# Two outlook-attention layers: channels dealt out as 3p+i over the partitions, and layer 1's results turned by VectorE in 32 by 32 pieces

## The chip, the cores and the metric

The kernel runs on one core of one Trainium2 chip, in float32 throughout. The metric is the device time of one execution in microseconds (us). The kernel is a single launch; weights are only reordered on the host.

## The reference

The input x is 8 images of 56 x 56 positions with 384 channels. Two layers follow each other, each with a residual.

```python
def _gn(v, G=32, eps=1e-5):                       # 32 groups of 12 channels
    g = v.reshape(B_, H_, W_, G, C_ // G)
    m = jnp.mean(g, axis=(1, 2, 4), keepdims=True)
    s = jnp.var(g, axis=(1, 2, 4), keepdims=True)
    return ((g - m) / jnp.sqrt(s + eps)).reshape(v.shape)

# layer 0, on x = _gn(x): 12 heads of 32 channels, 3 x 3 patches
v = einsum('bhwc,oc->bhwo', x, Wv)
attn = softmax(einsum('bhwc,oc->bhwo', x, Wa).reshape(b, n, 12, 9, 9) * 32 ** -0.5, axis=-1)
out = einsum('bnhpq,bnqhd->bnphd', attn, patches(v))   # 9 outputs per position ...
y = fold(out)                                          # ... added up where they overlap
x = x + einsum('bhwc,oc->bhwo', y, Wo)

# layer 1, on _gn(x): 6 heads of 64 channels, one output per position
a = softmax((x @ W_attn + b_attn).reshape(B, H * W, 6, 9), axis=-1)
y = einsum('bpKhd,bphK->bphd', patches(x @ W_v + b_v), a)
x = x + y @ W_proj + b_proj
```

## The kernel before

**Layout.** Images go in pairs: a column of a pair is 2 x 56 = 112 rows. Between the layers and for every projection, activations lie with channels on the partitions, 128 to each of three chunks (`NCH` = 3): channel 128i + p is on partition p of chunk i. The input and the output have channels innermost in DRAM, so a column is turned on the way in and on the way out.

**Layer 0** takes one column of one pair per step, 224 steps. In `stats_chunk` TensorE transposes the raw x of the next pair, four columns and one chunk at a time (`pt`, from `xr`), ScalarE copies the result to `xt`, VectorE takes `bn_stats`, and `xt` is kept in DRAM. `norm_params` makes scale and bias of a pair: `bn_aggr` over each chunk and image, then `over_groups` twice (the mean, then the variance), each a matrix product with `gmat`. A group of 12 channels straddles chunks, so `gmat` has a block for each neighbouring pair of chunks and each product is seven float32 matmuls, which the trace shows as 14 instructions. `normed` applies scale and bias with one instruction per chunk and image. `attend` projects to logits (three banks of 288 columns) and to values, `fold` and the DRAM tables `ztab` and `vtab` bring softmax weights and values into patch form, and `plan` queues for each patch column of 7 the contractions (`pc`), their copies to `yT` by ScalarE, and six `project_out` (two halves of columns by three chunks), whose results go to DRAM as layer 1's input together with their statistics.

**Layer 1** works on 32 groups of 7 columns (4 pairs of 8), one column per step. A step runs one job of a queue, then `attend` for its column (a matmul of 438 columns for logits and values, of which every eighth column has none, since 8 columns of 112 rows fill 7 tiles of 128), then one more job, then stores logits and values by DMAs from POOL. The order of the jobs is the order of the work on TensorE: every matmul is kept in program order, and in layer 1 VectorE's, ScalarE's and SP's instructions too. `weigh`, `share` and `move` make the softmax of a group and its patch form at steps 3, 4 and 5 of the next group. `fetch` (at step 0) reads the `z` and `vp` patches of the group before by DMAs from SP, and queues 14 jobs, due from step 3: for each of two images two pairs of contractions (`pc`, two tiles of PSUM, `NC` = 2), each followed by a job that turns one column back, then six `project_out`, the last three with a turn attached. `project_out` multiplies `yT` by the output weights into `po`, and VectorE adds bias and residual in place in `x1t`. `turn(m)` transposes the three chunks of one column of `x1t` with TensorE into PSUM, ScalarE copies the turned column to `ot`, and after columns 3 and 6 POOL issues the DMA to the output. Turns of columns 3 to 6 wait in the list `turning` until the next group's contractions.

**PSUM** [...] three `banks` in rotation, the tags `t`, `f` and `o`, and two for `c`. In layer 1 `attend` rotates over two of the `banks`, the third serves every second turn; `project_out` alternates between `o` and `f`, and `move` uses `f`.

**Helpers.** Line 118 is every matmul, line 121 every transpose, and line 133 every instruction recorded through `InOrder`, so in the profile they are told apart by their tiles.

Of the kernel before, what the change touches and what calls it, by code (L numbers as in the profile page):

```python
# [15 lines left out]
def two_outlook_layers(  # L16
# [81 lines left out]

    xf = x.rearrange("b y x c -> (b y) x c")
# [52 lines left out]
    near = [range(max(0, i - 1), min(NCH, i + 2)) for i in range(NCH)]  # L152
    gmat = [const.tile([P, len(near[i]), P], F32, name=f"gmat_{i}") for i in range(NCH)]
    with tc.tile_pool(name="ps_setup", bufs=2, space=PS) as ps_setup:
        gsel = yT_flat[:G, :C]
        gpsimd.memset(gsel, 1.0)
        gpsimd.affine_select(
            out=gsel, in_=gsel, compare_op=ALU.is_ge, fill=0.0,
            base=0, pattern=[[1, C]], channel_multiplier=-GC,
        )  # L160
        gpsimd.affine_select(
            out=gsel, in_=gsel, compare_op=ALU.is_ge, fill=0.0,
            base=GC - 1, pattern=[[-1, C]], channel_multiplier=GC,
        )
        for i in range(NCH):
            pg = ps_setup.tile([P, C], F32, tag="pg", name=f"pg_{i}")
            matmul(pg, gsel[:, i * P : (i + 1) * P], gsel, start=True, stop=True)
            lo, hi = near[i][0] * P, (near[i][-1] + 1) * P
            nc.vector.tensor_scalar_mul(gmat[i].rearrange("p j c -> p (j c)"), pg[:, lo:hi], 1.0 / GC)
# [93 lines left out]
    def weight(pool, src, n, name, queue=nc.sync):  # L263
        t = pool.tile([P, NCH, n], F32, name=name)
        queue.dma_start(t, src.rearrange("(i p) n -> p i n", p=P))
        return t

    def norm_params(st, name, params, key):

        mv = stat.tile([P, NCH, IMG, 2], F32, tag="mv", name=f"mv_{name}")  # L270

        def over_groups(src, what):
            pg = ps.tile([P, NCH, IMG], F32, tag="t", name=f"p{what}_{name}")
            for j in range(NCH):
                for i in near[j]:
                    matmul(
                        pg[:, j, :], gmat[i][:, j - near[i][0], :], src[:, i, :],
                        start=(i == near[j][0]), stop=(i == near[j][-1]),
                    )
            g = stat.tile([P, NCH, IMG], F32, tag=what, name=f"{what}_{name}")  # L280
            vector.tensor_copy(g, pg)
            return g

        for i in range(NCH):
            for b in range(IMG):
                vector.bn_aggr(mv[:, i, b, :], st[:, i, b, :, :])
        yield
        mean = over_groups(mv[:, :, :, 0], "gmean")

        part = stat.tile([P, NCH, IMG], F32, tag="part", name=f"part_{name}")  # L290
        vector.tensor_sub(part, mv[:, :, :, 0], mean)
        vector.tensor_mul(part, part, part)
        vector.tensor_add(part, part, mv[:, :, :, 1])
        yield
        var = over_groups(part, "gvar")
        std = stat.tile([P, NCH, IMG], F32, tag="std", name=f"std_{name}")
        scalar.activation(std, var, AF.Sqrt, bias=eps_t)
        scale = const.tile([P, NCH, IMG], F32, name=f"scale_{name}")
        vector.reciprocal(scale, std)
        bias = const.tile([P, NCH, IMG], F32, name=f"bias_{name}")  # L300
        vector.scalar_tensor_tensor(bias, mean, -1.0, scale, ALU.mult, ALU.mult)
        params[key] = scale, bias
        yield
# [90 lines left out]
    scalar.dma_start(bo_t, bo1.rearrange("(i p) -> p i", p=P))  # L394
# [25 lines left out]
    def layer0(late, pools):  # L420
# [22 lines left out]
        def stats_chunk(pair, blk, i):  # L443

            if blk == 0 and i == 0:
                stats[pair] = stat.tile([P, NCH, IMG, NBLK, 6], F32, tag="st0", name=f"st0_{pair}")
# [7 lines left out]
            for j in range(XB):  # L454
                transpose(pt[:, j, :], xr[:, j, i * P : (i + 1) * P], ident[:R, :R])
            scalar.copy(xt[:, i], pt)
            yield
            for b in range(IMG):
                vector.bn_stats(stats[pair][:, i, b, blk, :], xt[:, i, :, b * H : (b + 1) * H])
# [54 lines left out]
        for blk in range(NBLK):  # L514
# [5 lines left out]
            if blk == 1:  # L520
                wv_t = weight(fixed, wv0, C, "wv0_t", sync)
# [31 lines left out]
        scalar.dma_start(wn, wa0.rearrange("(i p) n -> p i n", p=P))  # L553
# [21 lines left out]
        def normed(g, chunks, whole=True, shared=True, both=False):  # L575

            scale, bias = params[g // NBLK]
            xin, to = xins[g], xns[g // 2 % 2]
            for i in chunks:
                for b in range(IMG):  # L580
                    rows = slice(b * H, (b + 1) * H)

                    def put(dst, src):
                        if both and b:
                            vector.tensor_scalar(
                                dst, src, scale[:, i, b : b + 1], bias[:, i, b : b + 1],
                                ALU.mult, ALU.add,
                            )
                            return
                        scalar.activation(  # L590
                            dst, src, AF.Identity,
                            bias=bias[:, i, b : b + 1], scale=scale[:, i, b : b + 1],
                        )

                    n = XB - g % 2
                    if whole:
                        put(to[:, i, g % 2 * XB : g % 2 * XB + n, rows], xin[:, i, :n, rows])
                    if shared and g % 2:
                        put(
                            to[:, i, :, R + b * PART : R + (b + 1) * PART],  # L600
                            xin[:, i, n, rows].rearrange("p (j y) -> p j y", j=NTILE),
                        )
# [188 lines left out]
        def plan(pair, px, first, second, last):  # L791
# [38 lines left out]
            if px == 0:  # L830
                st1s[pair] = stat.tile([P, NCH, IMG, 2 * NPX, 6], F32, tag="st1", name=f"st1_{pair}")

            def project_out(half, j):
# [11 lines left out]
                for b in range(IMG):  # L845
                    vector.bn_stats(
                        st1s[pair][:, j, b, 2 * px + half, :],
# [30 lines left out]
        def upkeep(step):  # L878

            pair, c = divmod(step, W)  # L880
            if pair == 0:
                if c == 1:
                    gpsimd.memset(wts, 0.0)
                if c == 3:
                    sync.dma_start(wo_t, wo0.rearrange("(i p) n -> p i n", p=P))
# [11 lines left out]
            if j < NCH and g < NPAIR * NBLK:  # L897
                normed(g, (j,))
            if step < NCH:
                normed(1, (step,), shared=False)  # L900
# [13 lines left out]
        for i in range(NCH):  # L914
            normed(0, (i,), both=True)
            normed(1, (i,), whole=False, both=True)
# [81 lines left out]
    def layer1(pools, base, last_of_layer0, late_w):  # L998
# [24 lines left out]
        def normed(g, m0, m1):  # L1023
# [4 lines left out]
            for lo, hi in ((first + m0, min(cut, first + m1)), (cut, first + m1)):  # L1028
# [3 lines left out]
                for i in range(NCH):  # L1032
                    for b in range(IMG):
                        rows = slice(b * H, (b + 1) * H)
                        scalar.activation(
                            to[:, i, :, rows], x1ts[g][:, i, lo - first : hi - first, rows],
                            AF.Identity,
                            bias=bias[:, i, b : b + 1], scale=scale[:, i, b : b + 1],
                        )
# [7 lines left out]
        nc.gpsimd.dma_start(wc_t[:, :, :NA1], wa1.rearrange("(i p) n -> p i n", p=P))  # L1047
        nc.gpsimd.dma_start(wc_t[:, :, NA1:], wv1.rearrange("(i p) n -> p i n", p=P))
# [4 lines left out]
        wo_t = weight(fixed, wo1, C, "wo1_t")  # L1053
# [3 lines left out]
        def attend(g, m):  # L1057
# [7 lines left out]
            pa = bank(P, 0, NC1, 2)  # L1065
# [77 lines left out]
        def fetch(g, due):  # L1143
# [10 lines left out]
            for b in range(IMG):  # L1154
# [20 lines left out]
                for t in range(0, (NPY1 + n_tile - 1) // n_tile, NC):  # L1175
                    jobs.add(due, lambda t=t, f=contract: [f(t + n) for n in range(NC)])

                    jobs.add(due, turning.pop(0) if turning else lambda: None)

            def project_out(half, j):  # L1180
                lo, hi = HALVES[half]
                n = (hi - lo) * R
                po = ps.tile([P, 4 * R], F32, tag="of"[(half * NCH + j) % 2], name=f"po1_{g}_{half}_{j}")
# [6 lines left out]
            def turn(m):  # L1190

                half = m // 4
                lo, hi = HALVES[half]
                if m == lo:
                    fetch.ot = io.tile([R, 4, C], F32, tag="ot", name=f"ot_{g}_{half}")
                pt = banks[-1][:R, :C] if m % 2 else ps.tile([R, C], F32, tag="t", name=f"pt1_{g}_{m}")
                for i in range(NCH):
                    transpose(pt[:, i * P : (i + 1) * P], x1t[:, i, m, :], ident)
                scalar.copy(fetch.ot[:, m - lo, :], pt)
                if m == hi - 1:  # L1200
                    nc.gpsimd.dma_start(  # L1201
                        of[pair * R : (pair + 1) * R, px * PX + lo : px * PX + hi, :],
                        fetch.ot[:, : hi - lo],
                    )

            out, back = project_out, turn
            for work_of in (
                (lambda: out(0, 0),), (lambda: out(0, 1),), (lambda: out(0, 2),),
# [96 lines left out]
```

## Time and profile before

| | us |
|---|---|
| runs (median of 3; lowest to highest) | 3314.91; 3310.96 to 3317.94 |
| the profiled execution's own time | 3315.84 |
| its span, first to last instruction | 3314.0 |
| TensorE busy with matmuls | 3183.7 |
| VectorE, ScalarE, POOL busy | 1870.4, 1366.3, 1565.1 |
| layer 1's transposes of results (312 + 234 + 72 + 54 instructions) | 51.5 + 38.6 + 12.0 + 8.9 |
| ScalarE's copies to `ot` (128 + 96) | 61.2 + 46.1 |
| matmuls `pgmean` and `pgvar` (112 + 112) | 17.7 + 20.3 |
| mean granted TensorE clock | 0.978 |

The profile is of one execution, and its 3314.0 us can be divided by engine, by line and by tile. PE is TensorE's matmuls, PEld its weight loads, DVE is VectorE, ACT is ScalarE, POOL is GpSimd, SP is SyncE, which only issues DMAs here. A row of the groups names line, engine, operation, output and inputs, shape and count; then busy time and the mean length of one in ns; then how long the engine had been idle before, and what ended the wait. Matmuls overlap: the length of one is more than the distance to the next one's start. The trace's timeline gives starts, and distances between starts are the price on TensorE.

### The profile page before, as it was taken

The page shows a single profiled execution, that of the slowest core. Times are in us where ns is not written, and L with a number is a line of the kernel's source. Part 1 is how long each engine was busy: PE and PEld are TensorE (multiplying, and loading weights), DVE is VectorE, ACT ScalarE, POOL GpSimd, SP SyncE. Part 2 cuts the span into 40 slices and gives each one's busy share as a digit, 9 for nine tenths or more (in the row PEclk, how much of TensorE's full clock was granted, in tenths as well). Part 3 has the DMA queues.
Part 4 walks back from the last instruction along what each step waited for, and adds up shares of the span by engine and source line. Part 5 has one row for each costly group of instructions (what it writes and reads, how often), then busy time and mean ns, then how long its engine had stood idle before and what let it go on. Part 6 is the DMA issues. An engine that isn't in the chain of part 4 may idle for free. (4 is left out here: it accounts for less than half of the span.)

```text
span 3314.0 us, 75237 instructions
## 1 busy us (share of the span) xinstructions
PE 3183.7 (96%) x28510; PEld 2186.6 (66%) x28510; DVE 1870.4 (56%) x4786; ACT 1366.3 (41%) x3749; POOL 1565.1 (47%) x2375
## 2 busy tenths in 40 slices
PE   7899999999999999999999999899999999999998
PEld 5567767776777667677666667556666666666665
DVE  5667776767777776777666677443333333333332
ACT  4444444444444444444343444234343443434432
POOL 2655555545555554455554555454343443434431
PEclk8899999999999999999999999899999999999999
DMA  9699988979897898899787888877778777787775
GB/s 294 201 308 295 303 274 270 292 258 304 300 315 235 279 308 266 290 294 300 229 257 259 288 253 294 285 240 212 220 215 233 212 216 226 220 222 214 223 215 155
DMA packets 554908, 850.99 MB, mean 257 GB/s; under 512 B 162174, under 2 KB 429954, under 8 KB 550450
## 3 DMA queue, kind: packets, MB, share of 16 engines
q1 hardware_dynamic: 448674, 672.76, 65.0%
q0 software_dynamic: 72016, 155.44, 14.7%
q10 hardware_dynamic: 33856, 17.98, 2.1%
q8 instruction: 225, 3.69, 0.5%
q14 instruction: 137, 1.12, 0.1%
HBM read 514.86 MB, written 322.17 MB: 253 GB/s over the span
## 5 line engine op out<-in xcount | busy, mean ns | idle before, releaser
L118 PE MATMUL bank<-wa_t,xn 128*128 128x288 f32 x3528 | 979.0, 415 | 3.5 <-ACT xn L133 2.1
L133 POOL TENSOR_TENSOR at<-at,den 128x972 f32<-128x972 f32 x196 | 440.5, 2247 | 859.3 <-DVE den L133 522.4
L118 PE MATMUL po<-yT,wo_t 128*128 128x448 f32 (+1 forms) x2304 | 821.0, 496 | 14.5 <-DVE x1t L133 12.0
L118 PEld LDWEIGHTS bank<-wa_t,xn 128*128 128x128 f32 x3528 | 652.9, 192 | 218.3 <-issue 22.2
L118 PEld LDWEIGHTS po<-yT,wo_t 128*128 128x128 f32 x2304 | 426.8, 191 | 296.0 <-issue 186.2
L133 ACT ACTIVATE at<-at 128x972 f32<-128x972 f32 (+1 forms) x228 | 215.8, 946 | 867.9 <-DVE at L133 860.5
L1075 POOL DMA_DIRECT2D at<-lgt x392 | 205.4, 527 | 616.3 <-DVE lgt L133 589.5
L118 PE MATMUL bank<-wc_t,xn 128*128 128x438 f32 x1176 | 477.8, 542 | 0.0
L133 DVE TENSOR_REDUCE mx<-bank 128x36 f32<-128x324 f32 x588 | 285.3, 485 | 340.6 <-PE bank L118 338.5
L118 PE MATMUL bank<-wv_t,xn 128*128 128x384 f32 x1176 | 417.3, 491 | 0.0
L118 PE MATMUL pc<-z,vp 121*32 121x49 f32 (+1 forms) x17664 | 374.7, 218 | 16.5 <-issue 10.3
L118 PEld LDWEIGHTS pc<-z,vp 121*32 121x32 f32 (+1 forms) x17664 | 337.8, 120 | 76.4 <-issue 51.0
L133 DVE TENSOR_TENSOR at<-bank,mx 128x324 f32<-128x324 f32 x588 | 291.4, 496 | 107.6 <-POOL pre L133 44.7
L118 PEld LDWEIGHTS bank<-wc_t,xn 128*128 128x128 f32 x1176 | 212.9, 190 | 169.4 <-issue 160.4
L118 PEld LDWEIGHTS bank<-wv_t,xn 128*128 128x128 f32 x1176 | 223.6, 192 | 134.8 <-issue 12.0
L133 DVE TENSOR_TENSOR lgt<-bank,ba_t 128x54 f32<-128x54 f32 x196 | 42.2, 215 | 455.8 <-PE bank L118 451.2
L133 POOL DMA_DIRECT2D vtab<-v x476 | 290.4, 614 | 14.4 <-issue 8.1
L133 ACT COPY yT<-pc 128x294 f32<-128x294 f32 (+2 forms) x512 | 195.7, 407 | 187.3 <-PE pc L118 186.4
L133 POOL TENSOR_TENSOR pre<-at,at 112x108 f32<-112x108 f32 (+1 forms) x440 | 224.4, 527 | 68.7 <-DMA at<-at 48.8
L133 DVE SCALAR_TENSOR_TENSOR x1t<-po,bo_t,x1t 128x448 f32<-128x448 f32 (+1 forms) x156 | 97.6, 626 | 249.5 <-PE po L118 249.5
L133 ACT COPY ot<-pt 112x384 f32<-112x384 f32 x128 | 61.2, 478 | 411.3 <-PE pt L121 411.0
L331 POOL DMA_DIRECT2D vtab<-v x392 | 211.4, 543 | 11.6 <-DMA vtab<-v 6.4
(118 smaller groups left out, 3279.0 us busy)
## 6 DMA issues: line engine op xcount, KB each, us to landing
z<-ztab SPq DMA_DIRECT2D x64, 2352.0 KB
vp<-vtab SPq DMA_DIRECT2D x64, 1536.0 KB
vp<-vtab SPq DMA_DIRECT2D x64, 945.0 KB
xres<-xT SPq DMA_DIRECT2D x32, 1176.0 KB
ztab<-wts SPq DMA_DIRECT2D x336, 110.2 KB
vtab<-v POOLq DMA_DIRECT2D x108, 336.0 KB, 6.2
xin<-xT SPq DMA_DIRECT2D x52, 672.0 KB
xr<-in_x SPq DMA_DIRECT2D x50, 672.0 KB
```

Source lines behind the costliest of these rows:

```text
L118: tc.keep_in_program_order(nc.tensor.matmul(*args, **kwargs))
L133: return lambda *args, **kwargs: tc.keep_in_program_order(op(*args, **kwargs))
L331: queue.dma_start(bass.AP(table.tensor, table.offset + first, [*([line * step, count] for step, count in rows_of or ((1, rows),)), *([[(R ...
L1075: nc.gpsimd.dma_start(at_of(g_of)[row : row + n, m_of].rearrange("r k h -> r (k h)"), lg[lo : lo + n])
```

## The change

Channels are dealt out differently: channel 3p + i lies on partition p of chunk i. Four partitions then hold one group of 12 channels in all three chunks.

- `gmat` becomes one 128 x 128 matrix, made by GpSimd alone; `over_groups` is one matmul; `bn_aggr` runs once for each image over all chunks; scale and bias have one value per partition and image.
- `normed` treats the three chunks in one instruction, in both layers.
- The transposes of raw x read every third channel (`xr[:, j, i::NCH]`).
- Weights are loaded by rows `(p i)`; the columns of the two output weights are sorted after loading, by VectorE in layer 0 (steps 5 to 7) and GpSimd in layer 1.
- In layer 1 `turn` goes. After each `project_out` VectorE transposes a chunk of four columns of `x1t` in 32 by 32 blocks into `ot`, and after the third chunk of a half POOL issues four DMAs, one for each quadrant of 32 partitions, with runs of 96 channels (384 bytes).
- The contractions are queued one by one, and the turn jobs between them go; a group still has 14 jobs. `attend` in layer 1 rotates over three banks, and `project_out` alternates between `o` and `t`.

```diff
+    def by_quadrant(ap, r0, col, n, b):
+        first = r0 * W * C + col * C + b * QC
+        return bass.AP(ap.tensor, ap.offset + first, [[C, n], [W * C, R], [1, QC]])
...
+    NPG = GC // NCH
+    gmat = const.tile([P, G, NPG], F32, name="gmat")
+    gpsimd.memset(gmat, 1.0 / NPG)
...
         def over_groups(src, what):
-            pg = ps.tile([P, NCH, IMG], F32, tag="t", name=f"p{what}_{name}")
-            for j in range(NCH):
-                for i in near[j]:
-                    matmul(
-                        pg[:, j, :], gmat[i][:, j - near[i][0], :], src[:, i, :],
-                        start=(i == near[j][0]), stop=(i == near[j][-1]),
-                    )
+            pg = ps.tile([P, IMG], F32, tag="t", name=f"p{what}_{name}")
+            matmul(pg, gmat, src, start=True, stop=True)
...
-        for i in range(NCH):
-            for b in range(IMG):
-                vector.bn_aggr(mv[:, i, b, :], st[:, i, b, :, :])
+        for b in range(IMG):
+            vector.bn_aggr(mv[:, b, :], st[:, b].rearrange("p i n s -> p (i n) s"))
...
-                transpose(pt[:, j, :], xr[:, j, i * P : (i + 1) * P], ident[:R, :R])
+                transpose(pt[:, j, :], xr[:, j, i::NCH], ident[:R, :R])
...
-                for i in range(NCH):
-                    for b in range(IMG):
-                        rows = slice(b * H, (b + 1) * H)
-                        scalar.activation(
-                            to[:, i, :, rows], x1ts[g][:, i, lo - first : hi - first, rows],
-                            AF.Identity,
-                            bias=bias[:, i, b : b + 1], scale=scale[:, i, b : b + 1],
-                        )
+                for b in range(IMG):
+                    rows = slice(b * H, (b + 1) * H)
+                    scalar.activation(
+                        to[:, :, :, rows], x1ts[g][:, :, lo - first : hi - first, rows],
+                        AF.Identity, bias=bias[:, b : b + 1], scale=scale[:, b : b + 1],
+                    )
...
-            pa = bank(P, 0, NC1, 2)
+            pa = bank(P, 0, NC1)
...
-                for t in range(0, (NPY1 + n_tile - 1) // n_tile, NC):
-                    jobs.add(due, lambda t=t, f=contract: [f(t + n) for n in range(NC)])
-
-                    jobs.add(due, turning.pop(0) if turning else lambda: None)
+                for t in range((NPY1 + n_tile - 1) // n_tile):
+                    jobs.add(due, lambda t=t, f=contract: f(t))
...
-                po = ps.tile([P, 4 * R], F32, tag="of"[(half * NCH + j) % 2], name=f"po1_{g}_{half}_{j}")
+                po = ps.tile([P, 4 * R], F32, tag="ot"[(half + j) % 2], name=f"po1_{g}_{half}_{j}")
...
-            def turn(m):
...
-                for i in range(NCH):
-                    transpose(pt[:, i * P : (i + 1) * P], x1t[:, i, m, :], ident)
-                scalar.copy(fetch.ot[:, m - lo, :], pt)
...
+                if j == 0:
+                    fetch.ot = io.tile([P, NB, QC], F32, tag="ot", name=f"ot_{g}_{half}")
+                vector.transpose(
+                    fetch.ot[:, :, j::NCH],
+                    x1t[:, j, hi - XB : hi].rearrange("p m r -> p (m r)").rearrange("p (k a) -> p a k", a=NB),
+                )
+                if j == NCH - 1:
+                    n = (hi - lo) * Q // XB
+                    for b in range(NQ):
+                        nc.gpsimd.dma_start(
+                            by_quadrant(out, pair * R, px * PX + lo, hi - lo, b),
+                            fetch.ot[(b + 1) * Q - n : (b + 1) * Q].rearrange("p a c -> p (a c)"),
+                        )
```

## The prediction

> **What bounds the kernel now.** I read the page's busy shares first, then TensorE's timeline inside one steady stretch of layer 1, then the groups of instructions kept apart by shape.
>
> ```profile
> PE 3183.7 (96%) x28510; PEld 2186.6 (66%) x28510; DVE 1870.4 (56%) x4786; ACT 1366.3 (41%) x3749; POOL 1565.1 (47%) x2375
> ```
>
> TensorE is busy 96% in both layers; no other engine is near. A saving counts where it takes TensorE time or a TensorE wait away. Layer 1 runs from about 2150 us to the end. Its timeline (start, length, matmul, count, idle before) shows how a step is paid:
>
> ```profile
> 2704.06 0.49 PE L121 MATMUL bank<-ident,x1t 128*112 128x128 f32 x3
> 2704.39 2.37 PE L118 MATMUL bank<-wc_t,xn 128*128 128x438 f32 x6
> 2706.60 1.86 PE L118 MATMUL po<-yT,wo_t 128*128 128x336 f32 x6
> 2708.29 0.49 PE L121 MATMUL pt<-ident,x1t 128*112 128x128 f32 x3
> 2708.72 1.61 PE L118 MATMUL pc<-z,vp 90*64 90x56 f32 x48
> 2710.26 2.47 PE L118 MATMUL bank<-wc_t,xn 128*128 128x438 f32 x6
> 2712.57 0.49 PE L121 MATMUL bank<-ident,x1t 128*112 128x128 f32 x3
> 2712.99 1.26 PE L118 MATMUL pc<-z,vp 90*64 90x56 f32 x36
> ```
>
> There is no idle time, so starts, not lengths, give the price. Three transposes take 0.33 us to the next start (2704.06 to 2704.39), and 0.43 when pc follows (2708.29 to 2708.72): entering pc costs 0.09. The same six bank matmuls take 2.21 after a transpose (2704.39 to 2706.60) and 2.31 after pc (2710.26 to 2712.57): leaving pc costs 0.10. So a burst of pc costs 0.2 beyond its matmuls.
>
> The group sums, once per normalisation, are in the same view of layer 0:
>
> ```profile
> 488.91 1.62 PE L118 MATMUL pgmean<-mv,gmat 128*128 128x2 f32 x14
> 490.39 2.50 PE L118 MATMUL po<-yT,wo_t 128*128 128x448 f32 x6
> ...
> 712.12 3.15 PE L118 MATMUL pgmean<-mv,gmat 128*128 128x2 f32 x14 [3.86 <-ACT xt L133]
> 715.13 1.12 PE L118 MATMUL pw<-pre,shift 112*112 112x120 f32 x4
> ```
>
> Fourteen matmuls of two columns take 1.48 us, or 3.01 after an idle stretch (the same count at half speed). Last, three rows by shape: TensorE's stats transposes, and two VectorE instructions over the same 378 elements, one with steps of 24 bytes, one contiguous:
>
> ```profile
> L121 PE MATMUL pt<-ident,xr 112*128 112x112 f32 x504 | 69.7, 260 | 7.4 <-DMA xr<-in_x 7.4
> L133 DVE TENSOR_REDUCE den<-at 112x42 f32<-112x378 f32 x32 | 26.9, 839 | 3.4 <-ACT at L133 3.4
> L133 DVE TENSOR_TENSOR at<-at,mx 112x378 f32<-112x378 f32 x32 | 17.7, 553 | 1.1
> ```
>
> [...] 1.48/14 is 106 ns, with two moving columns. [...] the reduce costs 0.29 us more than its contiguous neighbour, 0.76 ns an element. No row shows TensorE reading in steps of 12 bytes. [...]
>
> **The change part by part.**
>
> *Turning in layer 1.* A group of 7 columns has 21 transposes in 7 triples and 7 ScalarE copies of ot (478 ns each); they go. TensorE: 7 x 0.33 = 2.29 us a group. The jobs are recut: contractions were four bursts a group (48, 36, 48, 36), each followed by a turn job; now eight single jobs, two of which often touch. By the order of jobs in a step I count five bursts: +0.2. So -2.09.
>
> *A new wait.* The eighth contraction is now directly followed by the first project_out, with no attend between. It needs yT, copied by ScalarE from that contraction. Price: the end of the matmul (223 ns recorded, against a spacing of 33), the copy of 168 elements (307 ns), two hand-overs of about 40 ns: 0.57 us of TensorE idle a group. ScalarE could make it worse, since the copy stands behind the normalisation of the next group: now six activations in 2.64 us there, afterwards two or four longer ones. From their spacing (0.42 us for 168 elements, 0.38 for 112, so about 0.28 plus 0.83 ns an element) two of 504 take 1.4 us; they start some 2 us before the copy is due and are done. Only where no attend falls in that step (one group in eight) is the copy late by some 1.5 us more; I add 0.1. Queued behind the wait on TensorE is everything. Sum for layer 1: -2.09 + 0.67 = -1.42 us a group, x 32 = **-45 us**. Bounds: -67 with the wait covered, -25 with twice the wait.
>
> *VectorE's side.* Six transposes of 128x448 a group, read in steps of 56 bytes, written in steps of 12. Estimate: 553 ns for 378 elements gives about 0.61 for 448, plus 0.76 x 448 = 0.34: 0.95 us; 2 us if the write step is charged likewise. VectorE is busy 10.8 of 34 us there: 17 to 23 afterwards. A project_out takes TensorE 1.7 to 2.25 us and would take VectorE 0.6 + 0.95. Behind the transpose stand the additions that free the logits' banks, now three in rotation instead of two. Cost on the path: nothing; the cover goes at about 3.8 us per transpose.
>
> *The output's DMAs.* Two a group become eight, and runs of 4.6 or 6.1 KB become 3136 runs of 384 bytes. POOL: a vtab DMA takes 497 ns with 16 runs and about 700 with 224, so about 1 ns a run; 448 runs give 0.95 us. Eight take about 7 us instead of 1.1: POOL rises from 14 to 20 of 34 us. Behind them wait the stores of logits and v, 4 to 5 us later for two columns a group, with steps to spare. Transfer time: layer 0's 336-byte packets take 22 ns, so 25 ns each here, 4.9 us over 16 engines instead of 3.4. They also start earlier, in the stretch (2556 to 2567 us) where all DMA engines are full with z and vp; z lands at 2561.9 and pc starts at 2570.8, so a delay of 3 us is hidden by a margin of 8.9.
>
> *Group sums.* 28 matmuls become 2, six BATCH_NORM_AGGREGATE become two longer ones. After the start there are seven calls; their bursts add up to 32.1 us; 14 single ones at about 0.3 cost 4. Where the burst ran at half speed, the slow time moves to the next matmuls; I keep back 6: **-22 us** (-14 to -30).
>
> *Stats transposes.* The stationary side is now read with 12-byte steps. Four take 0.38 us (308.64 to 309.02 us), 96 ns each, set by 112 moving columns, with a weight load of about 106 mostly hidden: little slack. Bounds: nothing, or VectorE's 0.76 ns x 128 = 0.1 us each, x 504 = +50. [...] half the penalty may stay hidden: 40 ns, **+20 us**. The 168 of the first pair wait for x from DMA anyway.
>
> *Normalisation in one instruction for three chunks.* ScalarE saves about half its time on them, off the path: 0. *Start:* two bursts shrink (-5 us), but at 116.5 us TensorE idles 5.83 us for xr, whose queue is paced by DMA, and VectorE now sorts wo behind a DMA: **-1**, between -5 and +5. The layer-1 weight sort, three POOL copies near 2145 us, precedes a POOL pause of 9 us: 0. *End:* after the last matmul a transpose and four DMA issues stand where two turns, copies and one issue stood: **+2**.
>
> Sum: -45 - 22 + 20 - 1 + 2 = -46 us against the profiled execution's 3315.84 us (span 3314.0), giving 3270; the median of the runs is 0.9 lower, so 3269.
>
> **The rivals.**
> (a) *Weight loads don't mind the step, ScalarE's copy is covered.* -67 - 28 + 2 = -93: 3222. [...] Against: the copy's dependency is plain.
> (b) *The step costs in full and TensorE waits grow.* +50 - 25 - 22 + 1, or +4 at worst, -15 with the wait as forecast: 3300 to 3319. For it: the reduce at 839 ns.
> (c) *POOL becomes the bound of layer 1, slower.* If its work per run isn't in the recorded length, eight DMAs could take 3 us each: 24 + 12.7 = 36.7 us a group against 34.6: +2 x 32 + the rest = about 3360. It decides from (33 - 12.7)/8 = 2.5 us per DMA. For it: runs grow from some 2000 to 4900 a group. Against: landing times of POOL's small and large vtab DMAs hardly differ (5.9 us for 24 KB, 6.2 for 336 KB).
> (d) *The gain isn't made,* because another engine's wait fills TensorE's freed time: VectorE from 3.8 us per transpose. The 96% speak against it.
>
> **How the numbers follow.** Forecast 0.62; (a) 0.15; (b) 0.14, half of it within 0.2% (6.6 us, about what a measurement of this kernel can tell from no change); (c) and (d) 0.09. Faster: 0.62 + 0.15 + 0.03 = 0.80; same 0.07; slower 0.13. The range leaves out (c), the far half of (a) and the top of (b): 3225 to 3318.
>
> **What would show it.** Right: no pt or bank transposes of x1t; pc to po with an idle of about 0.5 us released by ACT yT; 32 groups some 1.4 us shorter; pgmean x2; a VectorE transpose near 1 us; POOL's out DMAs at about 1 us. Wrong: layer 0's four stats transposes at over 0.6 us, POOL over 80% busy in layer 1, pc waiting for z, VectorE in front of po.

## The result, and the profile after

The change makes the kernel slower: 3433.6 us median (3413.5 to 3454.8) against 3316.4 beside it, a ratio of 1.036 (95% interval 1.029 to 1.042). The forecast was 3269 us, within 3225 to 3318. The profiled execution of the changed kernel took 3437.73 us, its span is 3436.0. First the page's busy shares, as for the kernel before (busy us, share of the span, instructions):

```profile
PE 3151.4 (92%) x27640; PEld 2128.3 (62%) x27640; DVE 2048.5 (60%) x4942; ACT 1084.4 (32%) x2862; POOL 1817.4 (53%) x2570
```

TensorE has 870 matmuls less and is busy for 32 us less, but the span has grown by 122: the new time is idle time. The matmuls that are left also run slower where TensorE waits. The same steady stretch of layer 1, before and after (us; busy time and instructions of PE, PEld, DVE, ACT and POOL; then the granted TensorE clock, the mean busy share of the DMA engines, and GB/s):

```profile
2514.00:2792.00 278.00, 277.49 (x2160) 174.46 (x2156) 87.67 (x186) 112.21 (x328) 112.96 (x213) 1.00 0.78 220
...
2514.00:2792.00 278.00, 240.50 (x1724) 141.57 (x1723) 113.75 (x204) 55.19 (x162) 156.13 (x228) 0.94 0.85 193
```

Run 11 below has the same 27640 matmuls and is busy for 3103.0 us. Of the 180 us between its span and that of the change, 132 are idle time of TensorE and 48 are busy time at a lower clock. TensorE's timeline in layer 0, at the place where 14 instructions of `pgmean` took 1.48 us (start, length, matmul, count, idle before):

```profile
485.08 0.28 PE L127 MATMUL pgmean<-mv,gmat 128*128 128x2 f32 x2
485.22 2.50 PE L127 MATMUL po<-yT,wo_t 128*128 128x448 f32 x6
```

Two instructions take 0.14 us to the next start. The groups of instructions by shape (busy us, mean ns; then idle before) have the other rows shown of before, and the new one:

```profile
L142 DVE STREAM_TRANSPOSE ot<-x1t 128x448 f32<-128x448 f32 x156 | 151.0, 968 | 5.4
...
L130 PE MATMUL pt<-ident,xr 112*128 112x112 f32 x504 | 76.5, 274 | 5.4 <-DMA xr<-in_x 5.4
...
L142 DVE TENSOR_REDUCE den<-at 112x42 f32<-112x378 f32 x32 | 26.7, 835 | 2.3 <-ACT at L142 2.3
```

VectorE's transpose takes 968 ns, as estimated. A stats transpose is 14 ns longer (274 against 260). Layer 0 ends sooner: layer 1's first `bank` matmul starts at 2132.0 us instead of 2152.4. All of the loss lies in layer 1. There a group lasted 34.65 us on average before (mean over eight steady ones). After, 6 of 29 groups take 32.6 to 32.9 us, as the forecast had it; the others take 33.9 to 49, and the mean is 38.7: 4 us more a group, 116 us in these 29. The trace's list of waits (engine and tile that waited, what ended it, us in total, times, longest) says for what:

```profile
DVE lgt L142 <- DMA at<-lgt: 430.0, 61, 15.4
...
POOL out L1198 <- DMA out<-ot: 101.4, 61, 4.4
...
POOL at L1076 <- DMA out<-ot: 88.6, 45, 5.1
POOL vtab L328 <- DMA out<-ot: 87.5, 42, 6.2
```

In the kernel before, VectorE's wait for `at<-lgt` is 1.5 us in all, and POOL's `at` waits 6.3 us for outputs. TensorE's own waits in layer 1, from 2300 to 3050 us, first before and then after:

```profile
PE po L118 <- ACT yT L133: 1.5, 3, 0.5
...
PE po L127 <- DVE x1t L142: 62.0, 13, 11.2
PE po L127 <- DVE z L142: 17.8, 3, 8.8
```

One disturbed stretch of the timeline shows the chain:

```profile
2646.41 0.52 POOL L328 DMA_DIRECT2D vtab<-v  x1 [3.19 <-DMA out<-ot]
2646.85 0.21 DVE L142 TENSOR_TENSOR lgt<-bank,ba_t 128x54 f32<-128x54 f32 x1 [10.45 <-DMA at<-lgt]
...
2648.17 5.27 PE L127 MATMUL po<-yT,wo_t 128*128 128x336 f32 x12 [4.57 <-DVE x1t L142]
```

POOL cannot issue its next store until an output DMA has landed (in this trace its DMAs use eight semaphores in rotation, so each waits for the eighth before it). VectorE has waited 10.45 us for an older store to free a buffer of `lgt`; behind that wait stand the additions that drain `po`, and TensorE idles 4.57 us. The DMA view, for the same steady stretch of both kernels (2514 to 2788 us), gives the size and the median time from issue to landing. The kernel before:

```profile
out<-ot POOLq DMA_DIRECT2D x8, 672.0 KB, 7.8
out<-ot POOLq DMA_DIRECT2D x8, 504.0 KB, 5.0
```

The kernel after:

```profile
out<-ot POOLq DMA_DIRECT2D x28, 168.0 KB, 9.3
out<-ot POOLq DMA_DIRECT2D x30, 126.0 KB, 12.0
```

DMAs of a quarter of the size land later, and the smaller kind, three columns wide, lands last. That is the question of the experiments: what makes an output DMA land after 12 us?

### The profile page after: what moved, and what is told of

Same layout as the page of the kernel before. It is cut to its first block, busy times and chain, and to the rows that moved or that the text cites. A ratio compares the mean times of both kernels' runs of the same rounds, so it can differ in the third digit from the quotient of the medians.

```text
span 3436.0 us, 72742 instructions
## 1 busy us (share of the span) xinstructions
PE 3151.4 (92%) x27640; PEld 2128.3 (62%) x27640; DVE 2048.5 (60%) x4942; ACT 1084.4 (32%) x2862; POOL 1817.4 (53%) x2570
## 5 line engine op out<-in xcount | busy, mean ns | idle before, releaser
L127 PE MATMUL po<-yT,wo_t 128*128 128x448 f32 (+1 forms) x2304 | 861.4, 518 | 134.7 <-DVE x1t L142 88.9
L127 PEld LDWEIGHTS po<-yT,wo_t 128*128 128x128 f32 x2304 | 447.3, 199 | 452.6 <-issue 201.4
L127 PEld LDWEIGHTS pc<-z,vp 121*32 121x32 f32 (+1 forms) x17664 | 346.2, 121 | 138.6 <-issue 78.9
L127 PE MATMUL pc<-z,vp 121*32 121x49 f32 (+1 forms) x17664 | 386.4, 220 | 33.0 <-ACT yT L142 18.6
L1198 POOL DMA_DIRECT2D out<-ot x256 | 283.5, 1185 | 188.8 <-DMA out<-ot 101.4
L1076 POOL DMA_DIRECT2D at<-lgt x392 | 217.8, 581 | 180.2 <-DMA out<-ot 88.6
L142 ACT ACTIVATE wts<-pre,inside 112x48 f32<-112x48 f32 (+4 forms) x672 | 181.0, 358 | 66.8 <-POOL pre L142 34.2
```

The lines of the kernel that those rows point to most:

```text
L127: tc.keep_in_program_order(nc.tensor.matmul(*args, **kwargs))
L142: return lambda *args, **kwargs: tc.keep_in_program_order(op(*args, **kwargs))
L1076: nc.gpsimd.dma_start(at_of(g_of)[row : row + n, m_of].rearrange("r k h -> r (k h)"), lg[lo : lo + n])
L1198: nc.gpsimd.dma_start(by_quadrant(out, pair * R, px * PX + lo, hi - lo, b), fetch.ot[(b + 1) * Q - n : (b + 1) * Q].rearrange("p a c -> p ...
```

## The experiments

Three theories stood at the start, numbered as in the first expectations. **1, POOL's queue:** eight DMAs a group instead of two are too many, or land too late, and hold up the stores behind them. **2, short runs:** runs of 384 bytes use up the DMA engines, whoever issues them. **3, VectorE's transposes** stand in front of what TensorE waits for. Run 3 adds a fourth, **the shape of a DMA:** its access pattern gives it too few engines. Runs 2 to 7 write the pieces of the output to other places than the reference has them, with the same bytes in all. All ratios are to the kernel before, run on the same chip; its median there was 3313.9 to 3318.9 us, so differences between runs are good to a few us.

**1 (e1). Output DMAs from SP's queue.**

```diff
-                        nc.gpsimd.dma_start(
+                        sync.dma_start(
                             by_quadrant(out, pair * R, px * PX + lo, hi - lo, b),
```

> The kernel after, with the eight output DMAs of a group issued by SP instead of POOL; same runs, same engines' share. Theory 1 (POOL's DMAs: each waits for the one issued eight before it, the output's take 10.5 us to land, so the stores of logits and v come late and VectorE waits for free lgt tiles): the waits of VectorE for at<-lgt and of POOL for out<-ot go, layer 1's groups go from 38 us to the 32.8 of their undisturbed ones, about 3280 us. Theory 2 (runs of 384 bytes use up the DMA engines, whoever issues them): no gain, over 3400 us, and z and vp come late as well. Theory 3 (VectorE's transposes, 0.97 us each in its queue, are in front of what TensorE waits for): no gain, over 3400 us.

Measured: 3510.7 us (ratio 1.059, 1.057 to 1.061), slower still. VectorE's wait for `at<-lgt` is gone, so the stores are free; but SP's timeline reads

```profile
2611.22 13.75 SPq L142 DMA_DIRECT2D out<-ot  x4
2625.19 2.11 SPq L142 DMA_DIRECT2D vp<-vtab  x1
2627.36 2.81 SPq L142 DMA_DIRECT2D z<-ztab  x4
```

Four output DMAs occupy the queue for 13.75 us. The loads of `x1t` behind them come late (ScalarE's `xn` waits 151 us for them), and `yT`, which ScalarE makes after `xn`, with them: TensorE's `po` waits 184 us for it. Moving the DMAs moves the trouble; it is not in POOL alone.

**2 (e2). Long runs, and 3 (e3), short runs with many partitions outermost.** Both keep eight DMAs from POOL with the same bytes.

```diff
-                            by_quadrant(out, pair * R, px * PX + lo, hi - lo, b),
+ # 2:                        bass.AP(out.tensor, out.offset + at, [[size, n], [1, size]]),     size = 5376 bytes
+ # 3:                        bass.AP(out.tensor, out.offset + at, [[QC, n], [n * QC, NB], [1, QC]]),
```

> The kernel after, with the same eight output DMAs from POOL, each written as one run of 5376 bytes per partition to a wrong place in the output (the values are right, their order is not). Theory 1 in the form that the number of DMAs decides (32.5 a group at most eight in flight): little gain, 3380 us or more. Theory 1 in the form that their slow landing decides: landing falls from 10.5 to some 5 us and the time to about 3290 us. Theory 2 (short runs): about 3280 us. Theory 3 (VectorE): over 3400 us.

> The kernel after, with the same eight output DMAs from POOL and the same runs of 384 bytes, but with the partitions as the outer dimension on both sides, so that a DMA can be dealt out over more DMA engines than 4 or 3; the runs land in wrong places of the output. If it is the few engines of each DMA that make landing slow: landing falls from 10.5 to under 7 us, time below 3330 us. If it is the short runs themselves or the number of DMAs: no gain, over 3400 us.

Measured: 3254.8 us (0.981, 0.979 to 0.984) and 3258.7 (0.982, 0.980 to 0.984). Neither the number of DMAs nor the 384-byte runs is the cause, nor are VectorE's transposes, which both runs keep: with the same runs, but 32 or 24 instead of 4 or 3 as the outermost dimension in DRAM, the whole loss is gone and the gain there. In the change a DMA has 32 or 24 partitions in SBUF against 4 or 3 columns in DRAM; the author's estimate is that it goes over **four or three of the 16 DMA engines**, which the packet counts below bear out. But run 3 also wrote to one compact block instead of scattered rows.

**4 (e7). Few engines, compact, and 5 (e8), many engines, scattered** take the two apart.

```diff
+ # 4:      bass.AP(out.tensor, out.offset + at, [[QC, cols], [cols * QC, R], [1, QC]]),
+ # 5:      bass.AP(out.tensor, out.offset + at, [[W * C, n], [C, NB], [1, QC]]),
```

> The changed kernel with its eight output DMAs writing each quadrant into one compact block of DRAM, but still with a slowest dimension of 4 (or 3) columns on the DRAM side, as in the change; the output lands in other places than the reference's. The run before with wide access patterns (e3) differed from the change in two things: the number of DMA engines that share one DMA [...] and the scatter of the addresses. This kernel keeps the first, 4 or 3 engines, and takes the scatter away. Theory of few engines: no better than the change, 3400 us or more, out lands in 9 us or more, VectorE's lgt waits for at<-lgt DMAs some 400 us. Theory of scattered addresses: about 3260 us, landing 5.3 us.

> The mirror of the run before it: the changed kernel with its eight output DMAs of 384-byte runs scattered over the rows of the output as in the change, but with 32 (or 24) as the slowest dimension on both sides[...]; each run lands in another place than the reference's. Theory of few engines: about 3260 us, landing some 5.3 us, no wait of VectorE's lgt. Theory of scattered addresses: 3400 us or more, landing 9 us or more.

Measured: 3441.5 us (1.038, 1.035 to 1.041) and 3254.9 (0.981, 0.980 to 0.983). The slowest dimension alone gives the loss, and scattered addresses none of it.

That the number of engines goes with this dimension can be counted in the traces' records of single packets. In the change and in run 5 POOL's queue packs up to eleven runs of 384 bytes into a packet of 4224 bytes. Dealt to 4 or 3 engines, each takes 112 runs: ten such packets and a rest. The change writes 128 DMAs of either kind, so 128 x (40 + 30) = 8960 such packets are due, and its layer 1 has 8960. With 16 or 12 engines an engine takes 28 runs, two packets and a rest: 128 x (32 + 24) = 7168, and run 5 has 7168. Beside them stand packets of 44 bytes, 32000 in the change and 1024 in run 5. That is one for each such packet and each engine left out: 128 x (120 + 130) and 128 x 8. What they do is not shown. They aren't needed for the loss: run 1 has the same dimensions on SP's queue, with no packets of 44 bytes, and its ratio is 1.059.

**6 (e13). Eight engines.**

```diff
+           bass.AP(out.tensor, out.offset + at, [[QC, 8], [8 * QC, n * NB // 8], [1, QC]]),
```

> The changed kernel with its eight output DMAs written to compact blocks with 8 as the slowest dimension in DRAM (32 or 24 partitions in SBUF)[...]. The output lands in other places. Theory of few engines with a threshold: landing of some 6 to 7 us, POOL no longer blocked, 3255 to 3275 us. If the loss grows in proportion to the bytes on an engine: about 3310 us.

Measured: 3258.8 us (0.982, 0.981 to 0.984): no loss left. Runs 4 and 6 write the same compact blocks from the same source; only the way the block is cut into dimensions differs, 4 or 3 against 8 outermost. As 4 or 3 outermost count out to 4 or 3 engines in the change, eight is the author's estimate for run 6; POOL's queue records 14541 packets in it from 2514 to 2788 us, between run 4's 17641 and run 5's 12163. Eight outermost are enough here; the loss is not in proportion to the bytes that one engine would get, which the expectation put at 3310 us. Nor does the landing of the larger kind decide: in runs 2, 3, 5 and 6 a DMA of 168 KB lands after 8.0 to 8.7 us (median, 2514 to 2788 us), little under the change's 9.3. The smaller kind lands after 3.0 to 4.2 us instead of 12.0.

**7 (e12). Few engines in the kernel before.** Nothing of the change, but its order of dimensions.

```diff
-                        of[pair * R : (pair + 1) * R, px * PX + lo : px * PX + hi, :],
-                        fetch.ot[:, : hi - lo],
+                        bass.AP(of.tensor, of.offset + pair * R * W * C + (px * PX + lo) * C,
+                                [[C, hi - lo], [W * C, R], [1, C]]),
+                        fetch.ot[:, : hi - lo].rearrange("r m c -> r (m c)"),
```

> The kernel before, with nothing of the change but the shape of its two output DMAs a group: the DRAM side is written with 4 (or 3) columns as the slowest dimension instead of 112 rows, runs of 1536 bytes, the output lands in other places. [...] Theory of few engines: slower than before by tens of us, 3350 or more, landing of out at twice before's 7.5 us or more. Rival, it needs the eight DMAs of the change (two of eight in flight don't block POOL): within 0.5% of before, 3300 to 3333 us.

Measured: 3985.2 us (1.202, 1.200 to 1.205). Two DMAs a group are enough to lose 20%. The three-column half, 112 partitions against 3 columns, moves as if over one engine. The DMA view (busy share of the 16 engines in tenths and GB/s, 40 slices of 6.85 us; then the DMAs) shows it at work:

```profile
DMA  9950067796200952998006648991028589910195
GB/s 224 211 149 26 23 135 208 168 257 92 71 26 26 192 167 62 219 267 131 24 26 142 154 123 198 222 196 55 26 64 214 173 168 224 185 64 26 43 215 172
...
out<-ot POOLq DMA_DIRECT2D x5, 672.0 KB, 13.7
out<-ot POOLq DMA_DIRECT2D x4, 504.0 KB, 32.2
```

In stretches the engines together are under 10% busy and move 26 GB/s, as one engine of 16 would: from 2541 to 2545 us the packet records show one packet of 4608 bytes after another, 181 ns each. 504 KB at 26 GB/s are 19.8 us. No compute engine starts anything from 2530.5 to 2547.2 us; then POOL goes on:

```profile
2547.43 0.51 POOL L331 DMA_DIRECT2D vtab<-v  x1 [29.55 <-DMA at<-lgt]
```

It has waited 29.6 us for an `at<-lgt`, which moves at most 23.6 KB.

**8 (e11). More buffers for the logits**, to test the link that the waits of the change name.

```diff
-            lg = work.tile([P, NA1], F32, tag="lgt", name=f"lgt_{col}", bufs=4)
+            lg = work.tile([P, NA1], F32, tag="lgt", name=f"lgt_{col}", bufs=12)
```

> The change as it is, with 12 buffers for a column's logits (tile lgt) instead of 4. It tells whether these buffers are the link by which slow output DMAs reach TensorE: in the profile of the change VectorE's addition into lgt waits 430 us for DMA at<-lgt. Theory of the link: that wait goes, VectorE drains the banks in time, and at least half of the loss against wide output DMAs (3434 to 3256 us) comes back: 3345 us or less, with landing times of out still at 9 us or more. Rival, POOL's queue or the transfers themselves can't keep up, and the buffers only show it: 3400 us or more, with the wait moved to VectorE's mx or TensorE's pc (DMA z).

Measured: 3426.8 us (1.033, 1.029 to 1.037): the rival. The largest wait is gone and no time is won beyond the noise. The waits of VectorE now read

```profile
DVE mx L142 <- DMA at<-lgt: 120.1, 20, 15.6
...
DVE v L142 <- DMA vtab<-v: 100.4, 35, 8.8
```

The stores land late whatever waits for them; take one waiter away and the next (the softmax, the buffers of `v`) stops instead.

**9 (e15). The stores of logits and v from SP's queue**, in the change, **and 10 (e17), in the kernel of run 11**, as its control. Does the way lead through POOL's queue, or through the crowded engines?

```diff
-                    nc.gpsimd.dma_start(
+                    sync.dma_start(
                         at_of(g_of)[row : row + n, m_of].rearrange("r k h -> r (k h)"), lg[lo : lo + n]
...
-                    spread(nc.gpsimd, vtab1, SX1, ...)
+                    spread(sync, vtab1, SX1, ...)
```

> The change as it is (4 or 3 engines an output DMA, issued by POOL), but the stores of logits and v in layer 1 are issued by SP, so that nothing but the outputs stands in POOL's DMA queue. Theory of POOL's queue: the stores are free of the outputs, VectorE's waits for at<-lgt and vtab<-v go, 3255 to 3300 us. Theory of the engines: the transfers of every queue share the crowded engines, so the time stays at 3380 us or more, with the waits for at<-lgt, z or vp still there.

> The control for the run before it: rows on partitions (e9, 14 engines an output DMA, 3256 us) with the stores of logits and v issued by SP. If the place of the stores costs nothing by itself, 3250 to 3270 us by both theories; if SP's queue holds the stores or its loads up, more than 3290 us, and then the run before it has to be read against this one.

Measured: 3522.4 us (1.062, 1.059 to 1.064) and 3305.7 (0.997, 0.996 to 0.998). The place of the stores costs 50 us by itself (3305.7 against 3256.0), so run 9 is read against run 10: few engines cost 217 us with nothing but outputs in POOL's DMA queue of layer 1, against 178 with the stores there (3433.6 against 3256.0). TensorE's waits in run 9, from 2300 to 3050 us:

```profile
PE pc L127 <- DMA z<-ztab: 54.9, 8, 13.1
...
PE pc L127 <- DMA vp<-vtab: 21.3, 7, 5.6
```

In run 10 they are 18.4 us for `z` and 1.7 for `vp`. So POOL's queue is one way, not a needed one: with few engines, loads from SP's queue come late too. How the 178 us of the change divide between the two stays open.

**11 (e9). The change with rows on the partitions.** VectorE turns the pieces so that a partition of a quadrant holds rows 4k to 4k+3; a DMA then has 112 rows outermost in DRAM and 28 partitions in SBUF. By the author's count of its packets it goes over 14 engines; POOL's queue records 12388 packets from 2514 to 2788 us, near run 5's 12163 (17211 in the change).

```diff
                 vector.transpose(
-                    fetch.ot[:, :, j::NCH],
-                    x1t[:, j, hi - XB : hi].rearrange("p m r -> p (m r)").rearrange("p (k a) -> p a k", a=NB),
+                    fetch.ot[:, : RLO * cols, j::NCH].rearrange("p (a m) c -> p a m c", a=RLO),
+                    bass.AP(flat.tensor, flat.offset + first, [list(flat.ap[0]), [1, RLO], [R, cols], [RLO, Q]]),
...
-                            by_quadrant(out, pair * R, px * PX + lo, hi - lo, b),
-                            fetch.ot[(b + 1) * Q - n : (b + 1) * Q].rearrange("p a c -> p (a c)"),
+                            bass.AP(out.tensor, to, [[W * C, R], [C, cols], [1, QC]]),
+                            fetch.ot[b * Q + k0 : b * Q + k0 + NK, : RLO * cols].rearrange("p a c -> p (a c)"),
```

> The change, computing all of it, with another cut of the output: VectorE turns the pieces so that partition k of a quadrant holds rows 4k to 4k+3 (28 of 32 partitions are used, tile of 16 instead of 14 blocks, 512 or 384 elements instead of 448), and each output DMA has 112 rows as the slowest dimension in DRAM and 28 partitions in SBUF[...]. Theory of few engines: 3260 us (3250 to 3270), as the two runs with wide access patterns, VectorE's transpose at 1.05 to 1.1 us for 512 elements. If the scatter of the addresses counts, 3400 us or more; if both count, between.

Measured: 3256.0 us (0.981, 0.979 to 0.983), with the whole output written to its right place. From 2514 to 2788 us its DMAs land so:

```profile
out<-ot POOLq DMA_DIRECT2D x32, 168.0 KB, 6.9
...
out<-ot POOLq DMA_DIRECT2D x32, 126.0 KB, 3.0
```

**12 (e14). Run 11 with the outputs from SP**, the twin of run 1.

```diff
-                        nc.gpsimd.dma_start(
+                        sync.dma_start(
                             bass.AP(out.tensor, to, [[W * C, R], [C, cols], [1, QC]]),
```

> The kernel with rows on partitions (e9, 14 engines a DMA, 3256 us), its output DMAs issued by SP instead of POOL. With the change's shape the same move gave 3511 us, 77 us slower than on POOL. Theory: that loss was the few engines again [...], and the x1t loads stood behind the out DMAs in SP's queue: with 14 engines 3250 to 3275 us. Rival: SP's queue is the wrong place whatever the shape, since out waits there for VectorE's transpose with z, vp and x1t loads queued behind: 3300 us or more, with waits of ScalarE's xn for DMA x1t or of TensorE's pc for z.

Measured: 3250.8 us (0.980, 0.979 to 0.982). What lost 77 us against POOL with few engines loses nothing with 112 rows and 28 partitions outermost. In SP's timeline four output DMAs take 4.4 to 6.1 us, where run 1 had 13.75:

```profile
2599.94 4.44 SPq L144 DMA_DIRECT2D out<-ot  x4
```

**13 (e5). TensorE turns, the rest of the change stays:** layout, sums and normalisation, with before's jobs and its two output DMAs.

```diff
-                vector.transpose(fetch.ot[:, :, j::NCH], ...)
+                scalar.copy(fetch.ot[:, m - lo, :].rearrange("r (p i) -> r i p", i=NCH),
+                            pt.rearrange("r (i p) -> r i p", i=NCH))
```

> The kernel after, with layer 1's results turned by TensorE and the jobs of before (two DMAs of long runs a group); the new channel layout, the single group matmul and the merged normalisation stay. All three theories put the loss into the turning and its output: before less the 20 us by which layer 0 ends earlier in the trace after, about 3296 us. If the layout costs something in layer 1 (ScalarE's copy to ot now writes in steps of 12 bytes), up to 3320 us.

Measured: 3293.1 us (0.993, 0.991 to 0.996). The layout part is worth -21 us, the turning by VectorE with wide DMAs about another -37 (3256.0 in run 11).

**14 (e10). An attend ahead of the projection**, on run 11; and **15 (e16), the same with outputs from SP**.

```diff
...
-            jobs.run(base + step, 1)
+            jobs.run(base + step + 0.5, 1)
...
-                fetch(done - 1, base + step + 3)
+                fetch(done - 1, base + step + (3 if last else 3.5))
```

> The run before it (rows on partitions) with layer 1's jobs due half a step later, so that an attend lies between the last contraction and the first projection, and the eight contractions of a group lie in four pairs. By the working of the prediction the wait for yT (0.57 us a group) and one of five pc bursts (0.2) go: 0.8 us a group, 25 us in all: 3235 us (3228 to 3245). Rival: TensorE is then held by another wait (z late, VectorE's additions, the x1t loads), and less than 8 us are gained: 3252 to 3262.

> The best kernel so far (e10, rows on partitions and an attend ahead of the projection, 3225.5 us) with its output DMAs issued by SP, which gave 5 us (within the intervals) for e9. If that was real, 3220 us; if not, 3222 to 3230 us.

Measured: 3225.5 us (0.973, 0.971 to 0.974) and 3224.0 (0.972, 0.970 to 0.973); the outputs' queue makes no difference there. TensorE's timeline of run 14 at the seam:

```profile
2411.35 1.26 PE L129 MATMUL pc<-z,vp 90*64 90x56 f32 x36
2412.55 2.48 PE L129 MATMUL bank<-wc_t,xn 128*128 128x438 f32 x6
2414.86 8.62 PE L129 MATMUL po<-yT,wo_t 128*128 128x448 f32 x24
```

The attend covers the copy to `yT`; TensorE's waits for `yT` ahead of `po`, 11.7 us from 2300 to 3050 us in run 11, are 1.2. A group takes 32.35 us, and this kernel beats both: 2.7% under before, 6.1% under the change (3225.5 against 3433.6).

## Why the prediction was wrong

**The step that failed** is in the paragraph on the output's DMAs: "25 ns each here, 4.9 us over 16 engines instead of 3.4", and with it "a delay of 3 us is hidden by a margin of 8.9". The 25 ns are right: run 1's queue records each run as a packet of 384 bytes, and these take 25 ns on average. The 16 engines are wrong: the packets count out to four, or three. Over four engines, 448 runs are 112 each and, at 25 ns, an estimated 2.8 us of an engine's time instead of 0.7, on engines that all transfers together keep 85% busy in that stretch (mean of the 16). The forecast spread the whole group's bytes evenly and asked whether the sum fits; it took no account of when a single DMA lands and what waits for that. The margin was misread besides: 8.9 us is counted from `z`, but `pc` needs `vp` too, whose packets of 1536 bytes end at 2567.2 us in the profile before, 3.6 us ahead of `pc`. This did little harm: in the profile after, `pc` waits once for `vp`, 3.9 us, and never for `z`. Landing went to 9.3 and 12.0 us, and the "stores of logits and v, 4 to 5 us later ... with steps to spare" found no spare steps: VectorE waited up to 15.4 us for one of the four buffers of `lgt` (with twelve, the wait went elsewhere, run 8). Runs 3, 5 and 6 with many engines and runs 4 and 7 with few show the cause; run 11 removes it. How much of the delay each engine's load and each queue's order make up stays open.

**Rival (c)** had the right sign, and by luck the right engine: its reason was POOL's own work per run, deciding from 2.5 us a DMA. That work was 1.18 us (forecast 0.95), well below. POOL was 56% busy in layer 1's steady stretch (156.13 of 278 us) and waited for landings. (Its own terms add up to about 3380 us, not 3360.) Of the check "pc waiting for z, VectorE in front of po" the second half did show: `po` waits for VectorE's `x1t`, 62.0 us from 2300 to 3050 us.

**The rest of the sum**, with the DMAs made wide, was near: 3256.0 in run 11 against 3269.
- *Turning in layer 1:* -1.42 us a group forecast, -1.22 measured (34.65 to 33.43 us, run 11). The wait for `yT`, priced at 0.57, is 0.53 (11.7 us in 22 waits): 0.40 in seven groups of eight and 1.36 in the eighth. What was missed is what follows the long one: in three of four such groups of run 11 the granted clock is halved for 3.4 or 6.8 us from about the wait on, and they take 36.7 to 38.1 us; the fourth, at full clock, takes 35.0. Run 14 takes the wait and a burst of `pc` away and gains 1.08 a group (33.43 to 32.35), where the two were priced at 0.8; these groups then take 34.3.
- *VectorE's transpose:* 0.95 forecast, 968 ns measured, and hidden as said: in run 11, from 2300 to 3050 us, TensorE waits for `yT` alone. That the steps of the read make up 0.34 us of it is not shown: run 11 reads in steps of 16 bytes instead of 56, and its 881 and 1105 ns for 384 and 512 elements are no cheaper for each.
- *Group sums:* -22 forecast. The fourteen after the start take 4.1 us in the profile after, where they took 32.1: -28. Their price of about 4 was right, and the 6 us kept back were not needed.
- *Stats transposes:* +20 was mis-sized too. Four take 0.44 us (304.53 to 304.97 in the profile after) against 0.38: 15 ns each, about +7, not 40 ns. The weight load itself grew from 142 to 201 ns and stayed mostly hidden. The price was the author's estimate from a VectorE reduce with steps of six float32 (839 against 553 ns); no row showed TensorE reading in steps. Both terms together fit layer 0's end, 20 us sooner.
- *Start, normalisation:* not measured apart. Layout as a whole -21 (run 13) against -3.

The errors of 13 us (stats transposes) and 6 us (group sums) made the forecast cautious, and the turning gave some 6 us less; so the nearness to run 11 is in part that of errors that cancel. One uncounted number of engines outweighed them all.

## What to carry to other kernels

Before a DMA is priced, write down the outermost dimension of both of its sides, and count from its packets how many engines carry it: its bytes and runs are divided by that number, not by 16. Here 32 or 24 against 4 or 3 outermost counted out to 4 or 3 engines (8960 packets of 4224 bytes), 32 or 24 on both sides to 16 or 12 (7168). A store is hidden only if its landing is: ask which buffers it frees, how many there are, and what stands behind their waiter. When a rearranged store becomes slow, turn its dimensions round before changing its queue, its runs or its buffers; and once an engine's wait is named, see whether removing the waiter moves the time.

## What the runs showed of the hardware

- With 8, with 32 or 24, or with 112 outermost in DRAM, kernels with output runs of 384 bytes (3258.8, 3258.7 and 3256.0 us) are not measurably slower than one with runs of 5376 bytes (3254.8).
- POOL's queue records up to eleven runs of 384 bytes as one packet (4224 bytes, 228 ns in run 5, 313 in the change); SP's queue records each run alone (384 bytes, 24 ns in run 12).
- Issuing is longer too with a small outermost dimension in DRAM: with the same 448 or 336 runs of 384 bytes POOL spent 1185 ns on a DMA of the change (4 or 3 outermost), 813 in run 6 (8), 787 in run 11 (112) and 662 in run 5 (32 or 24).
- In run 7, with runs of 1536 bytes, the transfer that looks like one engine's alone moves 26 GB/s, one packet of 4608 bytes each 181 ns. Small stores issued beside such a DMA land late: the median of an `at<-lgt` of 23.6 KB is 23.1 us there, and 6.1 in the kernel before. Which engines a store has, the traces don't say.
- The change's output DMAs are worse on SP than on POOL (3510.7 against 3433.6 us). Why is not shown: no trace here numbers the engines.
- TensorE's granted clock was lower the more it idled. From 2514 to 2788 us it was busy for 273.5 of 274 us at 1.00 in the kernel before, 269.0 at 0.99 in run 11, 236.5 at 0.94 in the change, 227.4 at 0.91 in run 1 and 173.7 at 0.79 in run 7. In layer 1 of these kernels' steady groups single waits of 0.4 or 0.5 us left it at 1.00; around one of 1.36 us it was halved in three of four cases of run 11, and in two of four of run 3.
- VectorE's 32 by 32 transpose of float32 takes 881, 968 and 1105 ns for 384, 448 and 512 elements a partition, about 1.8 ns for each element more, with a result written in steps of 12 bytes.
